# Filling the bank of z's second half ahead of its sum, in a gated graph layer on one Trainium2 core

## The chip, the core and the metric

The kernel runs on one core of a Trainium2 chip. The core has five engines that run side by side, each with its own instruction queue: TensorE (PE in the profile, with its weight loads shown as PEld), VectorE (DVE), ScalarE (ACT), GpSimd (POOL) and SyncE (SP, which here only issues transfers). Matmuls write to PSUM, a small memory of eight banks; one bank holds 128 rows of 512 fp32 numbers. Everything else works on SBUF or moves between SBUF and main memory through DMA.

The metric is the device time of one execution in microseconds; lower is better. Where several runs are shown, their median counts.

## The reference

`x` is 16 batches of 1024 nodes with 256 features, `adj` a 1024 x 1024 matrix in which about nine entries in a row are not zero. Cut to what matters:

```python
pre_u = einsum('bud,dk->buk', h_t, W1[:d])
pre_v = einsum('bvd,dk->bvk', h_t, W1[d:])
hidden = relu(pre_u[:, :, None, :] + pre_v[:, None, :, :] + b1)
S = sigmoid(einsum('buvk,ko->buvo', hidden, W2)[..., 0] + b2[0])
a_t = einsum('buv,bud->bvd', S * A_a, h_t)
m_t = einsum('uv,bud->bvd', A_m, h_t) * h_t
z_t = beta1 * h_t + beta2 * (einsum('bvd,de->bve', a_t, Wa) + ba) \
    + beta3 * (einsum('bvd,de->bve', m_t, Wm) + bm)
```

Here `A_a = A_m = adj`, and the three betas are inputs. So each edge (u, v) of each batch gets a gate S, the neighbours of v are summed once with the gate and once without, and z is made of three terms: beta1 h, two matrix products, and a bias row `beta2 ba + beta3 bm`, which the kernel calls `bias`.

## The kernel before

**Blocks and steps.** The batches are cut into NG = 4 groups of 4, the nodes v into NT = 8 tiles of 128. One pair (group, tile) is a block: BS = 32 blocks, in the order of the list `order`; the last group has blocks 24 to 31. A block takes T = 10 steps, so there are 320 steps, `n`, with `k, s = divmod(n, T)`: the block and the step in it. In a step 128 edges of the tile are worked on for the four batches of the group.

**One step.** GpSimd gathers table rows of the neighbours, pre_u and h, into one of eight buffers `fetched` (L518). PE spreads pre_v + b1 over the edges into a bank pair `pc` (`expand`, L615). DVE adds the two (`add`, L648), then in `gate` multiplies by W2 under the relu and sums, one instruction for each batch (L656, four a step). ACT makes the sigmoid (L659) and scales the left operand with it (L661; L625 prepares it). PE sums the neighbours into accumulators (`aggregate`, L673), two steps at a time. `expand(n + 2)` needs the bank that `add(n)` has read.

**Once in a block.** Other work is laid between the steps by `products` and its callees. They share two PSUM banks through `small`, which takes them in turn:

- `halves(k + 1)`: pre_v + b1 of the next block in two halves of two batches (L449, L445), at s = 1 and 3 from n = 10 on; ACT copies each half out twice (L482, L483).
- `rows`: table rows of a later group, at s = 8 and s = 2 of the next block, up to n = 222 (L445, copied out in L461).
- `turn_over`: ACT has copied an accumulator to `ev` (L681); PE transposes it (L691), ACT copies it to `LT` (L694). At s = 8, 9, 0 and 2.
- `block_end(k - 1)`: z of the block before, in two halves, `h = 0` at s = 4 and 5, `h = 1` at s = 6 and 7. A half starts with the bias row as a matmul with `start=True` (`add_row`, L449), then the products with w_a and w_m (L722). Then, in most blocks, ACT copies the bank over `LT` (L736), DVE computes `hb = beta1 hb + z` (L737), and SP writes `hb` out. For `h = 1` of the last group PE adds beta1 h instead, as a product with a scaled identity (`be1_eye`, L726), and ACT copies the sum out (L728).

`hb` is h of the block, in two halves, loaded by SP at s = 5 and s = 7 of the block itself into one of four buffers `h_blk` (L921). So z of block k is made while block k + 1 runs, and h for its second half is loaded seven steps before step 4 of that.

**What sets the order.** Each engine runs its instructions in the order in which the program issues them; `after(step, f)` puts a call off to the end of a later step (`do(n)`, after `gate(n)`). Up to n = 229 (`n < LAST`) `expand` and `products` come ahead of `add` and `gate` in a step; from n = 230 on they come behind. `ROOM` is 10, `LISTS` is 110: up to there the lists of edges are still being made (`lists`), which also take banks from `small` and copy a flag tile `few` on GpSimd (L335).

The bias row is kept in two forms: `bias`, and `bias_p`, split into two parts for the matmul whose other operand is `unit`, a 128 x 128 tile of ones.

Of the kernel before, what the change touches and what calls it, by code (L numbers as in the profile page):

```python
# [7 lines left out]
FP = mybir.dt.float32  # L8
FR = mybir.dt.float32r
I32 = mybir.dt.int32  # L10
AF = mybir.ActivationFunctionType
ALU = mybir.AluOpType
AX = mybir.AxisListType
P = 128
# [3 lines left out]
def kernel(  # L18
# [42 lines left out]
    nc = tc.nc  # L61
    B, N, D = x.shape
    NT = N // P
    DC = D // P
    GB = 4
    NG = B // GB
# [4 lines left out]
    E = TW * P  # L71
# [17 lines left out]
    def load_rows(src, n, name, engine=nc.scalar, at_=None):  # L89
        t = const.tile([P, n], FP, name=name) if at_ is None else at_  # L90
        engine.dma_start(t, bass.AP(tensor=src.tensor, offset=src.offset, ap=[[0, P], [1, n]]))
        return t
# [8 lines left out]
    def fixed(shape, name, dt=FP):  # L101
        return const.tile(shape, dt, name=name)
# [9 lines left out]
    upto = fixed([P, E], "upto")  # L112
# [3 lines left out]
    row = rows32[:, 0:1]  # L116
# [62 lines left out]
    slot, nth = upto, upto[:, :S]  # L179


    unit = fixed([P, P], "unit", FR)
    nc.vector.tensor_scalar(unit, upto[:, :P], 0.0, None, ALU.is_ge)
    edge = fixed([P, 1], "edge")
    nc.vector.tensor_scalar(edge, inw, 0.0, None, ALU.is_equal)

# [6 lines left out]
    bias_p = fixed([P, D], "bias_p", FR)  # L193
# [12 lines left out]
    main = ctx.enter_context(ExitStack())  # L206
# [6 lines left out]
    lst = ExitStack()  # L213
    lists_done = lst.close
    lst = lst.enter_context(tc.tile_pool(name="lst", bufs=1))
    psc = main.enter_context(tc.tile_pool(name="psc", bufs=2, space=bass.MemoryType.PSUM))
    psa = main.enter_context(tc.tile_pool(name="psa", bufs=1, space=bass.MemoryType.PSUM))
    psm = main.enter_context(tc.tile_pool(name="psm", bufs=2, space=bass.MemoryType.PSUM))

    def small(name):  # L220
        return psm.tile([P, 512], FP, name="misc")


    def aside(vt):
# [17 lines left out]
    def lists(vt):  # L242
# [7 lines left out]
        for c in range(0, N, N if vt < EARLY else N // 2):  # L250
            c = slice(c, c + (N if vt < EARLY else N // 2))
# [36 lines left out]
        for i in range(4):  # L288
            nc.tensor.matmul(pw[:, i:i + 1], sums[:, i].rearrange("p w q v -> p (w q v)"), R[:, 0:1],
                             start=True, stop=True)  # L290
# [36 lines left out]
        nc.vector.tensor_tensor(thr[:, vt:vt + 1], last, none, ALU.add)  # L327
        yield "op"
        RR = lst.tile([P, NW, RC], FP, name="RR", bufs=2)
        few = lst.tile([P, E], mybir.dt.uint8, name="few", bufs=2)  # L330
        yield "slot"
        for w, mine in enumerate((soon, late)):
            nc.vector.tensor_scalar(RR[:, w, :], R, mine, None, ALU.mult)
# [68 lines left out]
    def after(step, f):  # L402
        due.setdefault(step, []).append(f)
# [41 lines left out]
                nc.tensor.matmul(p[:, bb * D:(bb + 1) * D], hT[:, 2 * h + bb, i, :], wt[:, i, :],  # L445
                                 start=(i == 0 and not begun), stop=(i == DC - 1), skip_group_check=begun)

    def add_row(p, parts):
        nc.tensor.matmul(p, unit, parts.unsqueeze(1).to_broadcast([P, 2, D]),  # L449
                         start=True, stop=False, skip_group_check=True)  # L450

    def rows(k, tab=None):

# [14 lines left out]

    cuts = {}

    def halves(k):
        X = cuts[k] = big.tile([P, NW, GD], FR, name="X")
        low = one.tile([P, GD], FP, name="low")
        for h in range(2):
            step = yield
            c = slice(2 * h * D, (2 * h + 2) * D)
            p = small("p")
            add_row(p, b1_p)  # L480
            half_product(p, hTs[order[k]], w_v, h, True)
            nc.scalar.copy(X[:, 0, c], p)  # L482
            nc.scalar.copy(low[:, c], p)  # L483
        after(step + (2 if k else 1), lambda: nc.vector.tensor_tensor(low, low, X[:, 0, :].bitcast(FP), ALU.subtract))  # L484
        yield
        nc.scalar.copy(X[W:, 1, :], X[W:, 0, :].bitcast(FP))
        for w in range(NW):
            yield
            nc.scalar.copy(X[(1 - w) * W:(2 - w) * W, w, :], low[w * W:(w + 1) * W])  # L489
# [46 lines left out]
    spare = spare_.rearrange("p b c n -> p b (c n)")  # L536
# [9 lines left out]
    marks, pcs, accs, evs, hbs, LTs, lefts = {}, {}, {}, {}, {}, {}, {}  # L546
# [12 lines left out]
    parts = halves(0)  # L559
    for t, turns_ in enumerate(script):  # L560
        step = t - 100
# [148 lines left out]
    def block_end(k):  # L710

        g, vt = order[k]
        hb = hbs[k]
        for h in range(2):
            for i, wt in ((1, w_a), (0, w_m)):
                step = yield
                if i:
                    pz = small("pz")
                    add_row(pz, bias_p)
                for bb in range(2):  # L720
                    for c in range(DC):
                        nc.tensor.matmul(pz[:, bb * D:(bb + 1) * D], LTs[k][:, 2 * h + bb, i if bb else 1 - i, c, :], wt[:, c, :],  # L722
                                         start=False, stop=(i == 0 and c == DC - 1), skip_group_check=True)
            if h == 1 and g == NG - 1:
                for bb in range(2):
                    nc.tensor.matmul(pz[:, bb * D:(bb + 1) * D], be1_eye[0], hb[h][:, bb, :], start=False, stop=True,  # L726
                                     skip_group_check=True)
                nc.scalar.copy(hb[h], pz.rearrange("p (b d) -> p b d", b=2))  # L728
                b = g * GB + 2 * h
                after(step + 2, lambda hb=hb[h], b=b: nc.sync.dma_start(  # L730
                    out[b:b + 2, vt * P:(vt + 1) * P, :].rearrange("b p d -> p b d"), hb))
                continue
            z = pz.rearrange("p (b d) -> p b d", b=2)
            if step >= ROOM:
                z = LTs[k][:, 2 * h].rearrange("p k c n -> p (k c n)").rearrange("p (b d) -> p b d", b=2)
                nc.scalar.copy(z, pz.rearrange("p (b d) -> p b d", b=2))  # L736
            after(step + 1, lambda hb=hb[h], z=z: nc.vector.scalar_tensor_tensor(hb, hb, be1, z, ALU.mult, ALU.add))  # L737
            b = g * GB + 2 * h
            after(step + 2, lambda hb=hb[h], b=b: nc.sync.dma_start(
                out[b:b + 2, vt * P:(vt + 1) * P, :].rearrange("b p d -> p b d"), hb))  # L740
        del hbs[k], LTs[k]
# [120 lines left out]
    ROOM, MORE, LISTS = 10, 3, 110  # L862
    LAST = (BS - NT - 1) * T
# [18 lines left out]
    for n in range(total + 2):  # L882
        k, s = divmod(n, T)
        if n < total - 3:
            last_in = n - 1 if n % 2 or n < ROOM else done
        else:
            last_in = n
        while done < min(last_in, total):
            gather_in(done)
            done += 1  # L890
        if n % TW == 1 and n // TW + 1 < total // TW:
            load_mark(n // TW + 1)
        if n < LAST:
            expand(n + 2)
            if n >= ROOM:
                fill(n, False)
            products(n, k, s)
        if n + 1 < total:
            add(n + 1)
        if n < total:  # L900
            gate(n)
            if n + 1 < total:
                left_adj(n + 1)
        do(n)
        if s == 8 and ROOM <= n < LAST:
            turn_over(k, 0, 0, n)
        if n >= LAST and n + 2 < total:
            expand(n + 2)
        if n == 1:
            bias = load_rows(bm, D, "bias", nc.sync, spare[:, 1])  # L910
            ba_b = load_rows(ba, D, "ba_b", nc.sync, spare[:, 2])
            be1 = load_rows(beta1, 1, "be1", nc.sync)
            be2 = load_rows(beta2, 1, "be2", nc.sync)
            be3 = load_rows(beta3, 1, "be3", nc.sync)
            after(10, scale_late)
        if s in (5, 7) and k < BS - 1:
            h = s // 7
            hb = big.tile([P, 2, D], FP, name="h_blk", bufs=4)
            hbs.setdefault(k, []).append(hb)
            g, vt = order[k]  # L920
            nc.sync.dma_start(hb.rearrange("p b d -> p (b d)"),  # L921
                              table[g][vt * P:(vt + 1) * P, GD + 2 * h * D:GD + (2 * h + 2) * D])
        if n == total - 6:
            hbs[BS - 1] = hT_free.pop(0).rearrange("p b c n -> p b (c n)")
            for v, m, f in tails:
                for h, o in tail_rows(x, v, m, f):
                    nc.sync.dma_start(h, o)
        for i in advance.get(n, ()):
            next(made[i], None)
        if n in start_list:  # L930
            running.append([made[start_list[n]], True, n])
            piece_of(running[-1], n)
        if n < ROOM or n >= LAST:
            fill(n, False)
        if n >= LAST:
            products(n, k, s)
        if n == LISTS:
            assert not running and all(next(x, None) is None for x in made)
            lists_done()
            more = main.enter_context(tc.tile_pool(name="more", bufs=1))  # L940
            hT_free.extend(hT_places(more, MORE, NH))
# [120 lines left out]
```

## Time and profile before

| | |
|---|---|
| three runs | 1077.29, 1075.63, 1071.70 us; median 1075.63 |
| profiled execution | 1082.24 us, of it 1080.4 us from the first to the last instruction |
| mean granted TensorE clock | 0.990 |
| TensorE busy | 1020.1 us (94%) |
| VectorE busy | 1017.6 us (94%) |
| ScalarE busy | 862.6 us (80%) |
| GpSimd busy | 459.3 us (43%) |
| L737, beta1 h + z on DVE | 55 times, 743 ns each |
| L726, matmuls with be1_eye | 28 times, 7.2 us in all |
| L736, L728, copies of z on ACT | 55 and 7 times, 582 and 566 ns each |
| L449, bias row of z | 62 times, 24.6 us in all |

How to read it: a line of the profile names the kernel's line, the engine, the operation, and the tiles, `out<-in`; then a count and durations. The shares of busy time are means over the whole run. A matmul of fp32 operands appears as two passes, each with its own weight load, which is why 14 matmuls with `be1_eye` show as 28. Two views are used below: the windows, which give each engine's busy time in a stretch of the run, and the timeline, which lists instructions with their start and length, and in brackets how long the engine stood idle before them and what ended that.

### The profile page before, as it was taken

The page shows a single profiled execution, that of the slowest core. Times are in us where ns is not written, and L with a number is a line of the kernel's source. Part 1 is how long each engine was busy: PE and PEld are TensorE (multiplying, and loading weights), DVE is VectorE, ACT ScalarE, POOL GpSimd, SP SyncE. Part 2 cuts the span into 40 slices and gives each one's busy share as a digit, 9 for nine tenths or more (in the row PEclk, how much of TensorE's full clock was granted, in tenths as well). Part 3 has the DMA queues.
Part 4 walks back from the last instruction along what each step waited for, and adds up shares of the span by engine and source line. Part 5 has one row for each costly group of instructions (what it writes and reads, how often), then busy time and mean ns, then how long its engine had stood idle before and what let it go on. Part 6 is the DMA issues. An engine that isn't in the chain of part 4 may idle for free.

```text
span 1080.4 us, 24120 instructions
## 1 busy us (share of the span) xinstructions
PE 1020.1 (94%) x7673; PEld 731.3 (68%) x7673; DVE 1017.6 (94%) x3481; ACT 862.6 (80%) x2616; POOL 459.3 (43%) x456
## 2 busy tenths in 40 slices
PE   7777999999999999999999999999999999999996
PEld 6654676776666776677777767777766667666654
DVE  8687999998999999999999999999999999999993
ACT  3246787788888887898888888889889889999983
POOL 2666676555257334553333334333333333333330
PEclk9989999999999999999999999999999999999999
DMA  9999899999999999999999999999999999999991
GB/s 283 327 340 385 313 339 381 362 382 378 403 352 371 408 381 385 379 403 395 404 393 399 412 384 392 408 396 389 381 361 370 369 348 368 365 381 369 365 341 44
DMA packets 147752, 394.56 MB, mean 365 GB/s; under 512 B 18224, under 2 KB 94512, under 8 KB 111408
## 3 DMA queue, kind: packets, MB, share of 16 engines
q0 software_dynamic: 50544, 301.16, 70.9%
q1 hardware_dynamic: 83776, 78.66, 22.9%
q10 hardware_dynamic: 13296, 13.11, 3.5%
q8 instruction: 63, 1.03, 0.4%
q14 instruction: 73, 0.60, 0.1%
HBM read 396.93 MB, written 50.33 MB: 414 GB/s over the span
## 4 chain that ended last, share of the span: by engine, by line
PE 40%; DVE 34%; issue 10%; ACT 8%; DMA 5%; POOL 2%; another core or an unknown queue 0%; POOLq 0%; DVEq 0%; ACTq 0%
DVE fetched L656 16%; DVE fetched L648 12%; PE acc L673 10%; PE misc L722 10%; PE misc L445 9%; PE pc L615 7%; DMA fetched<-table,uidx 3%; PE misc L691 2%; ACT left L661 2%; DVE LT L705 1%; ACT X L489 1%; PE misc L449 1%; DVE low L484 1%; DVE h_blk L737 1%; DMA hT__635<-in_xT_dram 1%
## 5 line engine op out<-in xcount | busy, mean ns | idle before, releaser
L518 POOL DMA_INDIRECT fetched<-table,uidx x320 | 339.4, 1061 | 529.0 <-PE acc L673 389.0
L656 DVE SCALAR_TENSOR_TENSOR fetched<-fetched,w_b 128x256 f32<-128x256 f32 x1280 | 478.0, 419 | 0.0
L648 DVE TENSOR_TENSOR fetched<-fetched,pc 128x1024 f32<-128x1024 f32 x320 | 387.7, 1212 | 29.9 <-PE pc L615 19.4
L661 ACT ACTIVATE left<-left,gt 128x32 f32<-128x32 f32 (+1 forms) x1280 | 299.6, 305 | 10.4
L673 PE MATMUL acc<-fetched,left 128*32 128x256 f32 x4096 | 273.4, 385 | 6.3 <-ACT gt L659 3.7
L615 PE MATMUL pc<-X,mark 128*128 128x512 f32 x640 | 243.7, 462 | 10.9 <-DVE fetched L648 9.3
L673 PEld LDWEIGHTS acc<-fetched,left 128*32 128x32 f32 x4096 | 127.6, 109 | 112.1 <-issue 29.1
L615 PEld LDWEIGHTS pc<-X,mark 128*128 128x128 f32 x640 | 105.4, 189 | 88.9 <-issue 41.6
L659 ACT ACTIVATE gt<-sc,b_b 128x4 f32<-128x4 f32 x320 | 95.9, 300 | 46.7 <-DVE fetched L656 37.5
L722 PE MATMUL misc<-w_m,LT 128*128 128x256 f32 x496 | 117.3, 379 | 0.0
L722 PE MATMUL misc<-w_a,LT 128*128 128x256 f32 x496 | 117.2, 379 | 0.0
L445 PE MATMUL misc<-w_v,hT 128*128 128x256 f32 x448 | 107.6, 383 | 0.0
L722 PEld LDWEIGHTS misc<-w_a,LT 128*128 128x128 f32 x496 | 93.8, 189 | 15.3 <-issue 0.4
L722 PEld LDWEIGHTS misc<-w_m,LT 128*128 128x128 f32 x496 | 93.8, 190 | 15.1
L625 ACT ACTIVATE left<-onehot,val 128x64 f32<-128x64 bf16 (+1 forms) x320 | 102.9, 322 | 0.0
L385 POOL DMA_INDIRECT val<-in_adjT_dram,vidx x80 | 87.2, 1090 | 34.4 <-issue 20.4
L656 DVE DVE_READ_ACCUMULATOR fetched<-fetched,w_b 128x1 f32 x1280 | 100.7, 79 | 0.0
L691 PE MATMUL misc<-ident,ev 128*128 128x128 f32 x512 | 79.5, 278 | 18.5 <-issue 7.0
L445 PEld LDWEIGHTS misc<-w_v,hT 128*128 128x128 f32 x448 | 86.4, 193 | 14.3
L691 PEld LDWEIGHTS misc<-ident,ev 128*128 128x128 f32 x512 | 60.7, 141 | 45.7 <-ACT ev L681 15.2
L482 ACT CAST X<-misc 128x512 fp32r<-128x512 f32 x64 | 37.1, 580 | 55.2 <-PE misc L445 48.0
L445 PE MATMUL misc<-w_u,hT 128*128 128x256 f32 x320 | 76.6, 386 | 4.0 <-issue 3.8
(185 smaller groups left out, 1011.3 us busy)
## 6 DMA issues: line engine op xcount, KB each, us to landing
h_blk<-table SPq DMA_DIRECT2D x62, 256.0 KB
out_dram<-h_blk SPq DMA_DIRECT2D x62, 256.0 KB
hT<-in_xT_dram SPq DMA_DIRECT2D x28, 512.0 KB
table<-in_x_dram ACTq DMA_DIRECT2D x24, 512.0 KB
table<-tab SPq DMA_DIRECT2D x48, 256.0 KB
fetched<-table,uidx POOLq DMA_INDIRECT x320
table<-in_x_dram SPq DMA_DIRECT2D x8, 512.0 KB
table<-fetched SPq DMA_DIRECT2D x8, 512.0 KB
```

The lines of the kernel that those rows point to most:

```text
L385: nc.gpsimd.indirect_dma_start(out=val[:, i, j:j + 1], out_offset=None, in_=adj_flat, in_offset=bass.IndirectOffsetOnAxis(ap=vidx[:, i, j: ...
L445: nc.tensor.matmul(p[:, bb * D:(bb + 1) * D], hT[:, 2 * h + bb, i, :], wt[:, i, :], start=(i == 0 and not begun), stop=(i == DC - 1), skip ...
L518: nc.gpsimd.indirect_dma_start(out=fetched[at_slot[n]], out_offset=None, in_=table[g], in_offset=bass.IndirectOffsetOnAxis(ap=uidx[:, vt * ...
L615: nc.tensor.matmul(pcs[n][:, c], marks[n // TW][:, j * P:(j + 1) * P], cuts[k][:, w, c], start=True, stop=True)
L625: nc.scalar.activation(lefts[n][:, :m, 1::GB, :], onehot[:, i, o:o + m, :].unsqueeze(2).to_broadcast([P, m, GB // 2, V]), AF.Copy, scale=v ...
L648: nc.vector.tensor_tensor(t, t, pcs.pop(n), ALU.add)
L656: nc.vector.scalar_tensor_tensor(t[:, b, :], t[:, b, :], 0.0, w2_b, ALU.max, ALU.mult, accum_out=sc[:, b:b + 1])
L659: nc.scalar.activation(gt, sc, AF.Sigmoid, bias=b2_b)
L661: nc.scalar.activation(lefts[n][:, :m, 2 * b, :], lefts[n][:, :m, 1 + b // 2 * GB, :], AF.Copy, scale=gt[:, b:b + 1])
L673: nc.tensor.matmul(accs[h][b * 2 * V:(b + 1) * 2 * V, r, :], left[:, i, 2 * b - b % 2:2 * b - b % 2 + 2].rearrange("p k v -> p (k v)"), f[ ...
L691: nc.tensor.transpose(pt[:, r, :, c, :], ev[:, r, c * P:(c + 1) * P], ident)
L722: nc.tensor.matmul(pz[:, bb * D:(bb + 1) * D], LTs[k][:, 2 * h + bb, i if bb else 1 - i, c, :], wt[:, c, :], start=False, stop=(i == 0 and ...
```

## The change

`halves` gets a last part, `seed_z`. After the second half-product of block k, from step 111 on, it takes the bank of that half-product again and has it written: up to step 229 by DVE at the end of the next step, with beta1 h + bias; from step 230 on by ACT at once, with beta1 h. The tile is kept in the list `kept` until `block_end` takes it for `h = 1`. `small` now counts the banks itself in `turn_of`, so that a kept bank is passed by; the pool has two names with one buffer each in place of one name with two. `block_end` chooses by `filled` whether the bias row is added by a matmul, with or without `start`, and how the sum is finished.

Three changes free the memory: `unit` is one column, read 128 times; `few` has one buffer in place of two; `bias` gets a tile of its own, since it is now read to the end of block 22, where before it lay in a buffer that is used again.

```diff
-    unit = fixed([P, P], "unit", FR)
-    nc.vector.tensor_scalar(unit, upto[:, :P], 0.0, None, ALU.is_ge)
+    unit_ = fixed([P, 1], "unit", FR)
+    nc.vector.tensor_scalar(unit_, row, 0.0, None, ALU.is_ge)
+    unit = unit_.to_broadcast([P, P])
...
-    psm = main.enter_context(tc.tile_pool(name="psm", bufs=2, space=bass.MemoryType.PSUM))
-
-    def small(name):
-        return psm.tile([P, 512], FP, name="misc")
+    psm = main.enter_context(tc.tile_pool(name="psm", bufs=1, space=bass.MemoryType.PSUM))
+    turn_of, kept = [0], []
+
+    def small(name, bank=None):
+        if bank is None:
+            bank = turn_of[0] = 1 - turn_of[0]
+            if kept and kept[0][0] == bank:
+                bank = turn_of[0] = 1 - bank
+        return psm.tile([P, 512], FP, name=f"misc{bank}")
...
-        few = lst.tile([P, E], mybir.dt.uint8, name="few", bufs=2)
+        few = lst.tile([P, E], mybir.dt.uint8, name="few", bufs=1)
...
-    def add_row(p, parts):
+    def add_row(p, parts, start=True):
         nc.tensor.matmul(p, unit, parts.unsqueeze(1).to_broadcast([P, 2, D]),
-                         start=True, stop=False, skip_group_check=True)
+                         start=start, stop=False, skip_group_check=True)
...
+    def seed_z(k, step):
+        bank = turn_of[0]
+        pz = small("pz", bank)
+        kept.append((bank, pz))
+
+        def write():
+            z, hb = pz.rearrange("p (b d) -> p b d", d=D), hbs[k][1]
+            if step >= LAST:
+                nc.scalar.activation(z, hb, AF.Copy, scale=be1)
+            else:
+                nc.vector.scalar_tensor_tensor(z, hb, be1, bias.unsqueeze(1).to_broadcast([P, 2, D]), ALU.mult, ALU.add)
+        if step >= LAST:
+            write()
+        else:
+            after(step + 1, write)
+
...
             nc.scalar.copy(low[:, c], p)
+            if h == 1 and k > 1 and (step > LISTS):
+                seed_z(k - 2, step)
...
                 if i:
-                    pz = small("pz")
-                    add_row(pz, bias_p)
+                    filled = h == 1 and kept
+                    pz = kept.pop()[1] if filled else small("pz")
+                    if not filled or step >= LAST + 6:
+                        add_row(pz, bias_p, not filled)
...
-            if h == 1 and g == NG - 1:
+            by_eye = g == NG - 1 and not filled
+            if by_eye:
                 for bb in range(2):
                     nc.tensor.matmul(pz[:, bb * D:(bb + 1) * D], be1_eye[0], hb[h][:, bb, :], start=False, stop=True,
                                      skip_group_check=True)
+            b = g * GB + 2 * h
+            if by_eye or filled:
                 nc.scalar.copy(hb[h], pz.rearrange("p (b d) -> p b d", b=2))
...
-            z = pz.rearrange("p (b d) -> p b d", b=2)
-            if step >= ROOM:
-                z = LTs[k][:, 2 * h].rearrange("p k c n -> p (k c n)").rearrange("p (b d) -> p b d", b=2)
-                nc.scalar.copy(z, pz.rearrange("p (b d) -> p b d", b=2))
-            after(step + 1, lambda hb=hb[h], z=z: nc.vector.scalar_tensor_tensor(hb, hb, be1, z, ALU.mult, ALU.add))
-            b = g * GB + 2 * h
+            else:
+                z = pz.rearrange("p (b d) -> p b d", b=2)
+                if step >= ROOM:
+                    z = LTs[k][:, 2 * h].rearrange("p k c n -> p (k c n)").rearrange("p (b d) -> p b d", b=2)
+                    nc.scalar.copy(z, pz.rearrange("p (b d) -> p b d", b=2))
+                after(step + 1, lambda hb=hb[h], z=z: nc.vector.scalar_tensor_tensor(hb, hb, be1, z, ALU.mult, ALU.add))
...
-            bias = load_rows(bm, D, "bias", nc.sync, spare[:, 1])
+            bias = load_rows(bm, D, "bias", nc.sync)
```

More of the change, by code (lines that the diff above doesn't have):

```diff
@@ L727, in block_end @@
                                      skip_group_check=True)
+            b = g * GB + 2 * h
+            if by_eye or filled:
                 nc.scalar.copy(hb[h], pz.rearrange("p (b d) -> p b d", b=2))
-                b = g * GB + 2 * h
-                after(step + 2, lambda hb=hb[h], b=b: nc.sync.dma_start(
-                    out[b:b + 2, vt * P:(vt + 1) * P, :].rearrange("b p d -> p b d"), hb))
-                continue
-            z = pz.rearrange("p (b d) -> p b d", b=2)
-            if step >= ROOM:
-                z = LTs[k][:, 2 * h].rearrange("p k c n -> p (k c n)").rearrange("p (b d) -> p b d", b=2)
-                nc.scalar.copy(z, pz.rearrange("p (b d) -> p b d", b=2))
-            after(step + 1, lambda hb=hb[h], z=z: nc.vector.scalar_tensor_tensor(hb, hb, be1, z, ALU.mult, ALU.add))
-            b = g * GB + 2 * h
+            else:
[4 more added lines that the diff above has]
+                after(step + 1, lambda hb=hb[h], z=z: nc.vector.scalar_tensor_tensor(hb, hb, be1, z, ALU.mult, ALU.add))
             after(step + 2, lambda hb=hb[h], b=b: nc.sync.dma_start(
```

## The prediction

> **What bounds the kernel now.** I read the busy time by stage first, because the page's shares (PE 94%, DVE 94%) average two regimes. The windows view cuts whole blocks (ten steps each) out of the run: blocks 16, 19, 27 and 29. Columns after the stretch: length, then busy us (and instructions) of PE, PEld, DVE, ACT, POOL, then clock, DMA share, GB/s.
>
> ```profile
> 591.70:621.90 30.20, 30.13 (x234) 21.95 (x233) 28.98 (x97) 26.36 (x82) 10.83 (x10) 1.00 1.03 410
> 683.30:713.50 30.20, 30.13 (x234) 21.83 (x233) 29.00 (x96) 26.36 (x82) 10.63 (x10) 1.00 1.02 400
> 918.90:947.10 28.20, 27.55 (x228) 19.60 (x223) 28.20 (x95) 25.63 (x80) 10.38 (x10) 1.00 0.96 360
> 975.30:1003.50 28.20, 27.59 (x228) 19.68 (x224) 28.20 (x95) 25.59 (x80) 10.12 (x10) 1.00 0.98 366
> ```
>
> In blocks 12 to 22 PE is idle 0.07 us of 30.2 and DVE 1.2 us: PE sets the period. In blocks 25 to 30 DVE is never idle and PE lacks 0.6 us: DVE sets it. The waits view agrees: in 471.4 to 773.7 DVE L648 waits 11.9 us for PE L615, in 862.4 to 1031.7 it waits for nothing.
>
> Then the timeline at the end of block 15, PE's weight loads and ACT's copies (start us, length):
>
> ```profile
> 590.27 0.59 ACT L736 COPY LT<-misc 128x512 f32<-128x512 f32 x1 [0.15 <-PE misc L722]
> ...
> 595.72 0.58 ACT L681 COPY ev<-acc 128x512 f32<-128x512 f32 x1
> ```
> ```profile
> 590.31 1.71 PEld L445 LDWEIGHTS misc<-w_u,hT__6826 128*128 128x128 f32 x8
> 592.04 0.57 PEld L691 LDWEIGHTS misc<-ident,ev 128*128 128x128 f32 x4
> ...
> 595.54 0.30 PEld L615 LDWEIGHTS pc<-X,mark 128*128 128x128 f32 x2
> 596.35 0.42 PEld L691 LDWEIGHTS misc<-ident,ev 128*128 128x128 f32 x4 [0.50 <-ACT ev L681]
> 596.94 0.16 PEld L673 LDWEIGHTS acc<-fetched,left 128*32 128x32 f32 x8 [0.17 <-issue]
> ```
>
> Two paths leave the end of z's second half (590.23). PE goes on with the next table rows (L445) at once, in the other bank, and reaches the transposes at about 595.86. ACT copies z out (L736), then works without a gap up to the copy of ev, which ends at 596.30. PE waits 0.5 us for it. So here ACT's path, not PE's own work, is the longer one, by half a microsecond.
>
> The same place in a DVE-bound block (end of 27):
>
> ```profile
> 944.12 0.84 PEld L726 LDWEIGHTS misc<-h_blk,be_eye 128*128 128x128 f32 x4
> 944.99 0.41 PEld L615 LDWEIGHTS pc<-X,mark 128*128 128x128 f32 x2
> 945.43 0.59 PEld L691 LDWEIGHTS misc<-ident,ev 128*128 128x128 f32 x4
> 946.19 1.45 PEld L673 LDWEIGHTS acc<-fetched,left 128*32 128x32 f32 x32 [0.17 <-issue]
> ...
> 950.30 0.42 PEld L691 LDWEIGHTS misc<-ident,ev 128*128 128x128 f32 x4 [1.04 <-ACT ev L681]
> 950.88 0.16 PEld L673 LDWEIGHTS acc<-fetched,left 128*32 128x32 f32 x8 [0.17 <-issue]
> ```
>
> **The change, part by part.**
>
> *What it does when built.* `filled = h == 1 and kept` names the list `kept` itself, not a truth value. The next line pops its only entry, so every later `not filled` is true. Hence the bias matmul is issued for both halves with start=True, over the seed; in the last group both halves, not one, go through be1_eye; the other blocks keep copy and L737. The instruction order of the built kernel says the same: 62 bias_p matmuls as before, be1_eye matmuls 14 to 28 (two passes each), L737 55 to 48, and beside them 12 new DVE and 8 new ACT writes into misc. The seeds are extra work that is thrown away. [...]
>
> *DVE seeds, blocks 11 to 22.* 128x512, two SBUF inputs, PSUM output. No row writes PSUM from DVE; nearest are L737 (0.743 us, 0.665 to the next start) and twice L648 per element, 1.21. I take 0.665 by form. It stands after step 4's gates, where DVE runs some 3.6 us ahead (L648 of 609.33 ends at 610.55 and frees the bank that PE takes at 614.23), and is hidden in the 1.2 us of idle; 0 us. Without that cover: 12 x 0.665 = 8.0 us. It also reads h four steps earlier than L737 did; the load for block 16 is issued at 591.5, its last packet ends at 609.7, and the seed would be due at 609.3. Up to a microsecond there, once; the others land 2.3 us or more before.
>
> *ACT seeds, blocks 23 to 30.* Nearest L728, 0.566 us. They follow the copies at 934.66, ahead of a gap of 0.67 us in which ACT waits for DVE: 0 us. Uncovered: 8 x 0.57 = 4.6.
>
> *The bank.* This is what I think costs most. `seed_z` keeps the bank of the second half-product for z, and turn_of stays on the other one. So the first `small` after z takes z's own bank, where before it took the other. It must wait until ACT has copied z out. The trace has this very wait once, in block 9, where the bookkeeping of the lists had turned the parity:
>
> ```profile
> 402.98 0.59 ACT L736 COPY LT<-misc 128x512 f32<-128x512 f32 x1 [0.67 <-PE misc L722]
> ...
> 403.61 1.59 PEld L445 LDWEIGHTS misc<-w_u,hT 128*128 128x128 f32 x8 [0.65 <-ACT LT L736]
> ```
>
> The weight load itself waits, and starts 0.05 after the copy. At 590.31 it would start at 590.86 + 0.05 = 590.91: 0.60 late. Eight loads after a wait take 1.63 us to the next one, against 1.73 unhindered, so the transposes come 0.49 late and reach the ev wait at 595.86 + 0.49 = 596.35: just when ev is ready. ACT's path starts at z's end and is not moved. What is left is the order in which loads and matmuls overlap: the matmul before the transposes ends 0.48 later (596.76), transposes end 0.44 behind it as at 595.38 to 595.82, and L673 loads at 597.12 instead of 596.94: 0.18. Blocks 11 to 22: 12 x 0.18 = **2.2 us**. Bounds: 0 if ACT's path swallows all, 12 x 0.60 = 7.2 if nothing is swallowed.
>
> [...] The row at 403.61 shows the load held with its matmul. [...]
>
> *Blocks 25 to 30 (z of 24 to 29).* DVE loses one L737: 28.20 - 0.665 = 27.54. PE gains four loads of be1_eye for the first half, 0.863 from the first to what follows (944.12 to 944.99). PE's own period now: the wait at 950.30 costs 0.83 (without it the transposes would end 0.44 after the matmul before them, which ends at 949.68, and L673 loads 0.07 ahead of that end: 950.05, not 950.88), so 28.20 - 0.83 = 27.37. New: 27.37 + 0.86 = 28.23, and the bank wait: z ends 945.36, copied 945.40 to 945.98, transposes load at 946.03 instead of 945.43, end 0.66 later at 946.69 instead of 946.26: 0.43. PE's period is 28.66. DVE's own way round (L648 to the gates 22.5, ACT to the end of the copy 2.1, PE to the next L615 3.2, hand-over 0.2) is 28.0, below. ev is then ready at 949.5 and no longer waited for. 28.66 - 28.20 = 0.46, six times: **2.8 us**. Bounds: 0.03 x 6 = 0.2 with the bank wait swallowed, and with only the 0.62 us of idle as slack (0.86 + 0.60 - 0.62) x 6 = 5.0.
>
> *Blocks 23, 24, 31.* In 23 and 24 ACT copies late (832.53, against a load at 830.41), but L615's next result is due at 836.12 and would be there at 835.8: 0. Block 31 gets be1_eye for both halves without a seed: 0.86 on PE, 0.47 of it ahead of a wait for ACT: 0.4; bounds 0 and 0.9.
>
> *The rest.* `unit` as one broadcast column: 0.18 us of DVE at 4.9 us goes; the load with step 0 has no row, all loads of 128 columns take 0.187 to 0.193, so 0. `few` with one buffer: the closest copies are 42.2 and 52.5, and the transfers between them end at 50.1: 0, 2.4 us spare. `bias` in a tile of its own: the same load and sum.
>
> **Sum:** 2.2 + 2.8 + 0.4 = 5.4 us on a span of 1080.4 (execution 1082.2). The runs' median, 1075.63, is 0.6% lower than that execution; the blocks are the same work, so 1075.6 + 5.4 = 1081.0. 0.5% (5.4 us) is about what can be told from no change, so the forecast sits on that line.
>
> **Rivals.**
> - *The bank wait passes on in full*: each block's PE path moves by 0.60 because ACT's path, which waits for PE at 590.27, moves too. 7.2 + 5.0 + 0.9 = 13.1: 1088.7. For: PE is idle only 0.07 us. Against: the 0.50 us wait for ev. 0.20.
> - *All is swallowed*: 0 + 0.2 + 0.4: 1076.2. For: ACT's path is the longer one now. Against: matmul order, and 0.86 more on PE against 0.83 of slack. 0.20.
> - *VectorE becomes the bound in 11 to 22* (slower): a seed that finds h late stops the gates behind it. Spare are 1.2 - 0.665 = 0.55 plus the 0.2 that PE loses, so from 0.75 us a block on it decides; at 1.5 us it adds 0.75 x 12 = 9.0: 1090. For: 609.7 against 609.3. Against: the other loads. 0.07.
> - *It does what its words say*: PE saves 0.23 (L449's pitch) and pays 0.18 in 12 blocks, -0.6; in 25 to 30 be1_eye only changes halves, PE 27.37 + 0.43 = 27.80, -0.4 x 6; -1 in 23 and 24: 1071.6. Against: the built order. 0.03.
>
> **How the numbers follow.** Forecast 0.50, own range 1078 to 1084, half of it under the line and half over. Slower by over 0.5%: 0.25 + 0.20 + 0.07 = 0.52. Within: 0.25 + 0.20 - 0.01 for scatter = 0.44. Faster: 0.03 + 0.01 = 0.04. The range goes from just under the swallowed case to the case in full: 1075 to 1089.
>
> **What would show it.** Right: in blocks 11 to 22 the first load after z waits some 0.6 us for ACT's copy of z, the ev wait shrinks from 0.5 to near 0, and the period goes from 30.13 to 30.3; in 25 to 30 DVE is idle again, about 1.1 us, and the period is 28.66; be1_eye matmuls 56; no wait before the DVE seeds. Wrong: periods of 30.7 (full), a period of 28.2 (swallowed), DVE waiting for a load of h_blk, or fewer bias_p matmuls than before.

## The result, and the profile after

The changed kernel is slower: 1092.75 us against 1077.02 us, medians of six runs each on one chip, ratio 1.0149 with a 95% interval of 1.0117 to 1.0181. That is 16 us where the prediction had 5.4, and outside its range of 1075 to 1089 us. The profiled execution of the changed kernel took 1095.94 us, of it 1094.1 from the first to the last instruction.

First the places that the prediction spoke of. The windows view of the changed kernel, blocks 16, 27 and 29, with the same columns as before:

```profile
600.00:630.20 30.20, 29.98 (x233) 21.85 (x232) 29.55 (x97) 26.35 (x82) 11.04 (x10) 1.00 1.02 407
927.30:957.20 29.90, 28.77 (x224) 20.48 (x224) 27.69 (x92) 26.11 (x81) 10.11 (x10) 1.00 0.95 346
986.00:1014.70 28.70, 28.48 (x224) 20.54 (x224) 27.78 (x94) 26.28 (x81) 9.92 (x10) 1.00 0.98 363
```

PE still sets the period in block 16, and now idles 0.2 us of it. In block 29 the period is 28.70 in place of 28.20, and DVE idles 0.9 us where it idled none: PE has taken over. (Block 27 has one disturbance more; 26, 28, 29 and 30 take 28.72, 28.75, 28.69 and 28.69.)

The timeline of the changed kernel at the end of block 15, and then at the end of block 28:

```profile
597.58 0.58 ACT L762 COPY LT<-misc 128x512 f32<-128x512 f32 x1 [0.15 <-PE misc L748]
598.21 1.59 PEld L451 LDWEIGHTS misc<-w_u,hT__6832 128*128 128x128 f32 x8 [0.64 <-ACT LT L762]
...
603.03 0.58 ACT L705 COPY ev<-acc 128x512 f32<-128x512 f32 x1
603.68 0.59 PEld L715 LDWEIGHTS misc<-ident,ev 128*128 128x128 f32 x4
```
```profile
984.24 0.84 PEld L753 LDWEIGHTS misc<-h_blk,be_eye 128*128 128x128 f32 x4
985.52 0.59 ACT L757 COPY h_blk<-misc 128x512 f32<-128x512 f32 x1
986.16 0.42 PEld L715 LDWEIGHTS misc<-ident,ev 128*128 128x128 f32 x4 [0.65 <-ACT h_blk L757]
```

Both show the wait for z's own bank. At 598.21 the load starts 0.05 us after ACT's copy (597.58 + 0.58), with 0.64 us of idling ahead of it, and the wait of 0.50 for `ev` further on is gone. At 986.16 the transposes wait 0.65 in the same way.

Now what the prediction did not have. PE's waits over the whole run of the changed kernel (line waited at, what for: us in all, times, longest) have two lines that the run before lacks at this size:

```profile
PE misc L451 <- DVE from L306: 7.9, 2, 5.1
PE misc L715 <- DVE from L306: 5.1, 1, 5.1
```

They fall in blocks 3, 6 and 9, while the lists of edges are still made. The timeline of the changed kernel in block 3 (PE, and one line of DVE):

```profile
177.85 0.95 PE L295 MATMUL misc<-R,sums 128*128 128x1 f32 x8
178.97 1.89 PE L451 MATMUL misc<-w_v,hT 128*128 128x256 f32 x8
...
186.21 0.16 DVE L306 TENSOR_TENSOR from<-misc,from 128x1 f32<-128x1 f32 x1
186.42 3.78 PE L451 MATMUL misc<-w_u,hT__1792 128*128 128x256 f32 x8 [5.10 <-DVE from L306]
```

L295 is the small product `pw` that the lists need. It holds one of the two banks until DVE has read it, in four instructions that make `from` and `first`, of which L306 is the last, at 186.21. (The profile's "wait for `from`" is the wait for this last one.) The half-product at 178.97 takes the other bank, and is soon copied out. The table row's product is next by strict turn on the bank of `pw`, though ACT has copied the other one out by 181.97. It waits 5.10 us. The same place in the kernel before:

```profile
182.86 0.95 PE L289 MATMUL misc<-R,sums 128*128 128x1 f32 x8
183.98 1.89 PE L445 MATMUL misc<-w_v,hT 128*128 128x256 f32 x8
188.53 1.99 PE L445 MATMUL misc<-w_u,hT__1791 128*128 128x256 f32 x8 [2.20 <-issue]
...
191.22 0.16 DVE L300 TENSOR_TENSOR from<-misc,from 128x1 f32<-128x1 f32 x1
```

There the third product runs at 188.53, 2.7 us ahead of the last read of `pw`. It can't be in that bank: the pool of two buffers under one name gave it the other one, and so passed the held one by.

The wait has a second price. In the changed kernel the eight matmuls at 186.42 take 3.78 us, where eight of the same size take 1.89 at 178.97. The windows view gives the granted clock (the column after POOL) around the wait:

```profile
172.30:185.00 12.70, 8.97 (x62) 6.36 (x60) 12.70 (x48) 9.77 (x32) 8.24 (x8) 1.00 1.02 383
186.40:190.20 3.80, 3.78 (x9) 2.96 (x10) 0.30 (x2) 0.00 (x0) 0.00 (x0) 0.50 0.57 193
190.20:200.00 9.80, 9.80 (x82) 6.39 (x81) 6.77 (x26) 6.59 (x20) 4.61 (x5) 0.88 0.79 245
```

Half the clock for 3.8 us and 0.88 for 9.8 more: 3.8 x 0.5 + 9.8 x 0.12 = 3.1 us of PE's work, lost on top of the wait.

A third thing is one seed. DVE's timeline in block 13 of the changed kernel:

```profile
527.35 0.76 DVE L487 SCALAR_TENSOR_TENSOR misc<-h_blk,be,bias 128x512 f32<-128x512 f32 x1 [5.89 <-DMA h_blk<-table]
```

The other eleven DVE seeds and the eight on ACT wait for no transfer.

### The profile page after: what moved, and what is told of

It reads as the page before. It is cut to its first block, busy times and chain, and to the rows that moved or that the text cites. A ratio compares the mean times of both kernels' runs of the same rounds, so it can differ in the third digit from the quotient of the medians.

```text
span 1094.1 us, 24217 instructions
## 1 busy us (share of the span) xinstructions
PE 1029.7 (94%) x7701; PEld 742.8 (68%) x7701; DVE 1022.1 (93%) x3486; ACT 868.4 (79%) x2624; POOL 462.3 (42%) x456
## 4 chain that ended last, share of the span: by engine, by line
PE 57%; DVE 23%; DMA 9%; issue 5%; ACT 4%; POOL 1%; ACTq 0%; SPq 0%; DVEq 0%; POOLq 0%
PE acc L697 15%; PE misc L451 14%; PE misc L748 12%; PE pc L639 9%; DVE fetched L680 9%; DVE fetched L672 7%; DMA fetched<-table,uidx 4%; PE misc L715 3%; DMA h_blk<-table 3%; PE misc L455 2%; ACT left L685 1%; DVE LT L729 1%; DVE low L508 1%; DMA hT__635<-in_xT_dram 1%; ACT LT L762 1%
## 5 line engine op out<-in xcount | busy, mean ns | idle before, releaser
L697 PE MATMUL acc<-fetched,left 128*32 128x256 f32 x4096 | 270.2, 386 | 3.4 <-ACT left L685 3.1
L639 PE MATMUL pc<-X,mark 128*128 128x512 f32 x640 | 244.2, 463 | 18.7 <-DVE fetched L672 18.6
L680 DVE DVE_READ_ACCUMULATOR fetched<-fetched,w_b 128x1 f32 x1280 | 109.5, 86 | 0.0
L715 PEld LDWEIGHTS misc<-ident,ev 128*128 128x128 f32 x512 | 63.3, 144 | 36.7 <-DVE from L306 5.6
```

The costliest lines, as they stand in the source:

```text
L639: nc.tensor.matmul(pcs[n][:, c], marks[n // TW][:, j * P:(j + 1) * P], cuts[k][:, w, c], start=True, stop=True)
L680: nc.vector.scalar_tensor_tensor(t[:, b, :], t[:, b, :], 0.0, w2_b, ALU.max, ALU.mult, accum_out=sc[:, b:b + 1])
L697: nc.tensor.matmul(accs[h][b * 2 * V:(b + 1) * 2 * V, r, :], left[:, i, 2 * b - b % 2:2 * b - b % 2 + 2].rearrange("p k v -> p (k v)"), f[ ...
L715: nc.tensor.transpose(pt[:, r, :, c, :], ev[:, r, c * P:(c + 1) * P], ident)
```

## The experiments

Each was run in five rounds beside the kernel before, whose median was 1076.5, 1075.9 and 1076.7 us in the three sets. Ratios are to the kernel before on the same chip.

| kernel | us | ratio, 95% interval |
|---|---|---|
| changed | 1092.75 | 1.0149 [1.0117, 1.0181] |
| small_only | 1082.78 | 1.0071 [1.0040, 1.0103] |
| noseed | 1085.56 | 1.0087 [1.0053, 1.0121] |
| eye2 | 1079.83 | 1.0038 [1.0011, 1.0064] |
| pool_seeds | 1079.29 | 1.0024 [0.9999, 1.0048] |
| e1_held | 1083.08 | 1.0053 [1.0026, 1.0080] |
| e5_turn | 1085.53 | 1.0087 [1.0062, 1.0111] |
| held_turn | 1078.55 | 1.0016 [0.9988, 1.0045] |
| e6_earlyh | 1088.53 | 1.0103 [1.0072, 1.0135] |
| pool_noseed | 1076.73 | 1.0000 [0.9973, 1.0027] |
| e4_bool | 1087.09 | 1.0098 [1.0063, 1.0133] |
| pool_bool | 1072.15 | 0.9958 [0.9929, 0.9987] |
| pool_bool_earlyh | 1073.48 | 0.9961 [0.9937, 0.9984] |

Block periods in us (start of the add in step 0 to that of the next block; for block 31 to the end of DVE's last instruction), read from the timelines of one execution each:

| block | before | changed | small_only | e1_held | e5_turn | held_turn | pool_bool |
|---|---|---|---|---|---|---|---|
| 3 | 35.20 | 40.15 | 39.21 | 33.68 | 39.47 | 34.82 | 33.67 |
| 6 | 33.59 | 35.41 | 35.02 | 33.56 | 35.39 | 33.64 | 33.61 |
| 10 | 34.01 | 36.34 | 36.34 | 34.02 | 36.33 | 33.13 | 33.13 |
| 13 | 30.66 | 35.73 | 30.42 | 36.58 | 32.80 | 30.77 | 34.00 |
| 20 | 30.13 | 30.21 | 30.26 | 30.23 | 30.13 | 30.16 | 29.90 |
| 29 | 28.24 | 28.69 | 28.20 | 28.69 | 28.27 | 28.27 | 27.61 |
| 31 | 41.95 | 43.84 | 41.94 | 43.25 | 42.84 | 42.86 | 42.33 |

### The turn alone: small_only

The kernel before, with only the strict turn:

```diff
-    psm = main.enter_context(tc.tile_pool(name="psm", bufs=2, space=bass.MemoryType.PSUM))
+    psm = main.enter_context(tc.tile_pool(name="psm", bufs=1, space=bass.MemoryType.PSUM))
+    turn_of = [0]
     def small(name):
-        return psm.tile([P, 512], FP, name="misc")
+        bank = turn_of[0] = 1 - turn_of[0]
+        return psm.tile([P, 512], FP, name=f"misc{bank}")
```

> The kernel before with nothing but the new counting of the two banks (two names with one buffer each, taken strictly in turn). Theory A (the lists' small product keeps its bank until VectorE has read it; the pool passed such a bank by, the strict turn runs into it): TensorE waits for VectorE's 'from' instructions, over 10 us in all against 1 to 2 before, mostly in blocks 3, 6 and 9, the granted clock falls below 0.985, blocks 12 to 30 keep their periods (30.1 and 28.2 us), and the time is 4 to 8 us over before. Rival B (the early blocks of the changed kernel were slower by chance): no such waits, within 3 us of before.

It costs 7.6 us (0.71% of 1076.5) with no seed, no be1_eye and no kept bank. The timeline has the same waits, and behind them a granted clock of 0.50 and 0.54 over 3.5 us (3.78 and 1.11 us for what takes 1.89 and 0.60 to 0.66):

```profile
185.25 3.78 PE L447 MATMUL misc<-w_u,hT__1791 128*128 128x256 f32 x8 [5.09 <-DVE from L302]
281.67 1.11 PE L693 MATMUL misc<-ident,ev 128*128 128x128 f32 x4 [5.14 <-DVE from L302]
```

Blocks 12 to 30 are as before. Half of the loss thus comes from a part of the change whose cost the prediction never worked out.

### No seeds: noseed

The changed kernel without the call of `seed_z`; no bank is kept, and the bias matmul starts every sum.

```diff
-            if h == 1 and k > 1 and (step > LISTS):
-                seed_z(k - 2, step)
```

> The changed kernel without seeds: the bank isn't kept, nothing is written ahead; the strict turn, be1_eye for both halves of the last group, unit, few and bias stay. Theory A with my own sums for the rest: small_only plus 0 to 1 us (blocks 25 to 30 at 28.2 to 28.3 us: TensorE 28.23, VectorE 27.54), blocks 12 to 22 at 30.1, no VectorE wait for h_blk; 4 to 9 us over before, so 7 to 11 us under the changed kernel. Rival (be1_eye is the cost): blocks 25 to 30 stay at 28.7, 3 us more than small_only.

The waits for `from` stay (5.1, 5.1 and 2.9 us). Block 29 comes back to 28.26, so be1_eye for both halves costs 0.02 to 0.06 a block there (28.20 to 28.24 before) and the rest of the 0.45 is z's bank. Seeds and z's bank together are 1.0149 - 1.0087 = 0.6%, some 6.7 us. Over before that leaves 9.4 us, just outside the 4 to 9 that I expected.

### be1_eye for both halves: eye2

The kernel before, with one condition changed:

```diff
-            if h == 1 and g == NG - 1:
+            if g == NG - 1:
```

> The kernel before with be1_eye for both halves of the last group. My sum: TensorE's period 27.37 + 0.86 = 28.23, VectorE's 27.54, so 28.2 us as before and 0 to 1 us in all. Rival (0.62 us of idle is all the slack there is): 28.4 to 28.5, 1.5 us and more; with 0.4 us for block 31 about 2 us.

By its ratio 1 to 7 us; by its periods less: 0.05 to 0.1 in most of blocks 25 to 30, and 0.9 in block 31 (42.86 for 41.95). pool_noseed below has the same edit and reads 1.0000. Between 0 and 4 us it stays open.

### The seeds with the old pool: pool_seeds

The changed kernel with the pool of before. No second tile is taken: the seed goes into the half-product's own tile, which holds its bank until z is done.

```diff
-    def seed_z(k, step):
-        bank = turn_of[0]
-        pz = small("pz", bank)
-        kept.append((bank, pz))
+    def seed_z(k, step, pz):
+        kept.append((0, pz))
```

> The changed kernel with the old pool of two buffers: the seed goes into the half-product's own tile, which the pool then keeps. Every bank is as in the kernel before, and the seeds are still overwritten. Theory A: no waits for 'from' beyond those of before, no wait for the copy of z, so blocks 12 to 22 at 30.1 and 25 to 30 at 28.2 to 28.3; what is left is be1_eye (0 to 1 us) and a VectorE wait for a late h_blk (0 to 6 us, in one block): 0 to 7 us over before. Rival C (the seeds' own time on VectorE counts): 12 x 0.665 = 8 us and more, periods of 30.8 in blocks 12 to 22.

With the banks as before, all seeds, the 28 more passes of be1_eye and the thrown-away work come to 0.24%, which the interval can't tell from nothing. No wait of PE's matmuls for `from` is over 0.6 us, and block 29 takes 28.27. Its profile has a wait of another kind, in block 13, to which pool_noseed returns.

### The held bank passed by: e1_held

The first experiments could still be read as a matter of which bank comes first. This one keeps the strict turn, changes its parity, and passes by the bank of `pw` alone:

```diff
-            if kept and kept[0][0] == bank:
+            if kept and kept[0][0] == bank or bank in taken:
                 bank = turn_of[0] = 1 - bank
...
         pw = aside(vt)
+        if vt >= EARLY - 1:
+            taken.append(turn_of[0])
...
         nc.vector.tensor_tensor(from_, pw[:, 3:4], from_, ALU.max)
+        taken.clear()
```

> The changed kernel, but `small` also passes by the bank of the lists' product `pw` until VectorE's `from` instructions have read it, as the old pool did. Theory A (in the list phase the strict turn runs into that bank): PE's waits for `from` (5.1 us in block 3, 5.1 in block 6, 2.8 in block 9) go, blocks 3, 6 and 10 come back to about 33.9, 33.6 and 33.3 us, and the time is 1085 us, 5 to 9 under the changed kernel, ratio to before 1.006 to 1.010; what is left is the bank of z and be1_eye. Rival B (it is not the held bank but that the order of banks differs at all, or the clock): the waits stay or turn up at other products, and the time stays at 1091 to 1094.

1.0149 becomes 1.0053: about 10 us back. The timeline in block 3 shows the row's product 4.2 us ahead of the last read of `pw`:

```profile
177.00 0.95 PE L297 MATMUL misc<-R,sums 128*128 128x1 f32 x8
178.12 1.89 PE L454 MATMUL misc<-w_v,hT 128*128 128x256 f32 x8
181.17 1.99 PE L454 MATMUL misc<-w_u,hT__1792 128*128 128x256 f32 x8 [0.70 <-ACT low L508]
...
185.37 0.15 DVE L308 TENSOR_TENSOR from<-misc,from 128x1 f32<-128x1 f32 x1
```

Eight matmuls take 1.99 us; the granted clock from 171.5 to 205.2 us is 1.00. Block 3 gives back 6.5 us: the wait is 4.4 shorter (0.70 for 5.10), and the 3.1 us that the clock had cost are more than the 2.1 left. The rival falls.

### z's bank alone: e5_turn

```diff
-                    pz = kept.pop()[1] if filled else small("pz")
+                    if filled:
+                        turn_of[0], pz = kept.pop()
+                    else:
+                        pz = small("pz")
```

> The changed kernel, but when the kept bank is taken for z, the turn moves with it, so that the first `small` after z gets the other bank and not z's own. Blocks 0 to 10 stay as in the changed kernel (waits for `from` of 5 us and all). Theory A: PE no longer waits for ACT's copy of z; blocks 25 to 30 go from 28.7 to 28.27, blocks 11 to 22 from 30.2 to 30.1, together 4 to 5 us with blocks 23, 24 and 31: 1088 us. Rival B (the last 7 us between the kernel without seeds and the changed one are the seeds' own cost, not z's bank): periods stay at 28.7 and 30.2, and the time stays at 1091 to 1094.

1.0087, some 6.7 us under the changed kernel, more than the 4 to 5 that I expected. The windows view, block 29:

```profile
976.00:1004.30 28.30, 28.30 (x227) 20.39 (x226) 27.81 (x94) 26.33 (x81) 10.20 (x10) 1.00 0.98 370
```

28.27 in place of 28.69, and block 20 back to 30.13. Blocks 26, 28, 29 and 30 give back 0.43 to 0.62 us each, and 20 to 22 give back 0.1 to 0.2 each. Not all of the difference between these two profiles is z's bank: of the 4.9 us in blocks 11 to 22, 2.9 lie in block 13, where the seed waited 2.9 us for h and not 5.9; and the 0.9 us in 23 and 24 together (58.9 to 58.0) are not there in e1_held, whose z's bank is taken in the same way and which needs 57.7.

### Both repairs of the banks: held_turn

> The changed kernel with both repairs of the banks: `small` passes by the bank of `pw` until `from` has read it, and the turn moves with the kept bank. If the two costs are separate places of the run, they add: the list phase gave back 9.6 thousandths and the turn 6.2, so 1.0149 - 0.0158 = 0.999, at most 1.003: 1075 to 1079 us, what is left being be1_eye for both halves and the late h in block 13. Rival (the two repairs reach the same wait, or the second one is scatter): 1.005 as with the first alone, 1081 to 1083.

1.0016, as the sum of the two demands; no difference from before can be told. The two places are separate, and they hold nearly all of the loss. With `pw`'s bank passed by in both, e1_held and held_turn differ by z's bank alone: 1.0053 - 1.0016 = 0.4%, 4 us.

### h loaded early: e6_earlyh

```diff
-        if s in (5, 7) and k < BS - 1:
-            h = s // 7
+        for h in range(2 * (s == 5 and k < BS - 1)):
```

> The changed kernel, but both halves of h are loaded at s = 5, not the second at s = 7. Theory A (the seed reads h before it has landed, once, in block 13): the wait of 5.9 us before the seed goes, block 13 comes from 35.7 back to some 30 to 31, and the time is 3 to 6 us under the changed kernel, 1087 to 1090. Rival B (SP's queue is behind at 500 us whatever stands in it): the wait moves to the load of hT, which now stands behind that of h, block 13 stays at 33 to 40 and the time at 1091 to 1095.

1.0103, 4 to 5 us under the changed kernel, though the intervals overlap. The windows view of block 13, first in the changed kernel, then here:

```profile
504.80:540.50 35.70, 32.08 (x243) 22.67 (x238) 29.81 (x100) 26.73 (x82) 10.90 (x10) 0.95 1.02 387
```
```profile
498.90:528.60 29.70, 29.49 (x231) 21.56 (x224) 29.70 (x100) 25.90 (x80) 10.55 (x10) 1.00 1.04 406
```

DVE idles 5.9 us in the first and not at all in the second. The late seed also cost PE its clock (0.95). That a seed waits for h here is no chance: 5.9, 6.7, 2.9 and 3.4 us in block 13 of the changed kernel, e1_held, e5_turn and e4_bool, and 6.6 us, a block later, in held_turn.

### The old pool without seeds: pool_noseed

The edits of pool_seeds to the pool, and no call of `seed_z`: of the change only be1_eye, `unit`, `few` and `bias` are left.

> The changed kernel with the old pool and without the call of seed_z: what is left of the change is be1_eye for both halves in the last group, the column `unit`, one buffer for `few` and a tile for `bias`. Theory A (the seeds bring late transfers in block 13, be1_eye costs 0.07 a block): block 13 at 30 to 31 with no wait over 1.5 us for hT, blocks 25 to 30 at 28.27, 1076 to 1080 us, 1.000 to 1.004. Rival B (the waits of block 13 belong to the earlier arrival at 490 us, not to the seeds): block 13 at 34 to 40 here too.

1.0000: those four edits cost nothing that can be measured. But my theory of block 13 missed: it takes 41.5 us here, without any seed. PE waits for hT, as in pool_seeds; PE's waits in the whole run of this kernel, then of that one:

```profile
PE misc L447 <- DMA hT<-in_xT_dram: 9.0, 1, 9.0
```
```profile
PE misc L447 <- DMA hT<-in_xT_dram: 9.3, 1, 9.3
```

Around 490 to 500 us SP's queue is behind in kernels that load h at s = 7: the issue of the second half of h in block 12, where most such issues take 0.3 to 0.5 us, takes 8.7 us before and in the changed kernel, 12.7 in noseed and 18.0 in small_only. With the seeds, the first to feel it is often the seed, which needs h four steps earlier than L737 did; without them it can be PE, which needs hT, or nobody (30.2 and 30.4 in eye2 and small_only). Which it is differs from kernel to kernel, and one execution of each is not enough to say why.

### As the words say: e4_bool, pool_bool, pool_bool_earlyh

```diff
-                    filled = h == 1 and kept
+                    filled = h == 1 and bool(kept)
```

e4_bool has this edit alone, pool_bool has it with the pool of pool_seeds, pool_bool_earlyh also has both halves of h loaded at s = 5.

> The changed kernel with `filled` as a truth value, so that the seed stands: no bias matmul for the second half up to step 235, be1_eye for the first half alone in the last group, no copy and no beta1 h + z for the second halves. Strict turn as in the changed kernel. By the prediction's terms: blocks 11 to 22 30.13 - 0.23 + 0.18 = 30.1; blocks 25 to 30 27.8 to 28.0 in place of 28.7; the list phase keeps its 7.6 us. Sum: 1076.5 + 7.6 - 0.5 - 1.8 = 1082, ratio 1.003 to 1.008, some 10 us under the changed kernel. Rival: the thrown-away seeds and matmuls cost nothing beside the banks, then it stays above 1088.

1.0098, not 1.003 to 1.008: 5 us under the changed kernel, half of what I expected. Both waits for a bank are still there, and the second grew. The timeline at the end of block 28:

```profile
977.24 0.56 ACT L757 COPY h_blk<-misc 128x512 f32<-128x512 f32 x1
977.85 0.42 PEld L715 LDWEIGHTS misc<-ident,ev 128*128 128x128 f32 x4 [1.27 <-ACT h_blk L757]
```

Without be1_eye after it z ends sooner, at 976.55, but ACT still has the left operand of a gate to scale (0.96 us from 976.13) and copies z at 977.24. The load waits 1.27 where it waited 0.65, and block 29 takes 28.53.

> The change as its words say, `filled` as a truth value, with the old pool of two buffers under one name (the seed is put into the second half-product's own tile). Theory A (the idea itself pays once the banks are left as they were): banks free as before, no waits for `from`, no wait for the copy of z. Blocks 11 to 22 at 29.9 (30.13 less the bias matmul's 0.23), blocks 25 to 30 at 27.5 to 28.0, together -4 to -6 us: 1071 to 1073, ratio 0.994 to 0.997. Rival B (VectorE or ScalarE sets the period as soon as PE gives way, or transfers come late as in block 13): periods as before, 30.1 and 28.2, and the time is 1075 to 1079, not told from before.

The ratio is 0.9958: faster than before, by 1 to 8 us, and some 20 us under the changed kernel. The windows view, blocks 19 and 28:

```profile
674.20:704.10 29.90, 29.83 (x233) 21.70 (x232) 28.95 (x98) 26.23 (x82) 11.05 (x10) 1.00 1.01 394
934.80:962.40 27.60, 26.64 (x212) 19.05 (x204) 27.60 (x94) 26.19 (x81) 10.15 (x10) 1.00 0.99 373
```

29.90 is 30.13 less the 0.23 of the bias matmul, as expected. 27.60 is 28.20 less L737 (27.54 with its 0.665), with DVE never idle: DVE sets it as before. Blocks 25, 28 and 29 take that; 26, 27 and 30 take 28.1 to 28.6 in this execution.

In e4_bool and pool_bool the second halves have no bias matmul with `start=True`, and z comes out right: the products added to what DVE or ACT had written. A matmul had just written every element of that bank in both kernels (`misc<-b_p,unit`, 128x512, of the half-product); over such a bank the seed counted.

> The change as its words say with the old pool, and both halves of h loaded at s = 5. If late h is a real term, block 13 goes from 34.0 to about 30 and the time to 1067 to 1070 us, 0.991 to 0.994. Rival (in that kernel the wait of block 13 is PE's, 4.3 us for hT, which then stands behind h in SP's queue): 1072 to 1077, 0.996 to 1.000.

Block 13 came from 34.00 to 29.95, as the first theory has it, but the median did not follow (0.9961 and 0.9958). What a single execution shows of block 13 is no measure of the runs' median here, and the expectation missed.

## Why the prediction was right and wrong

**Right: what the change does when built.** After the change be1_eye has 56 passes, L763 (L737 before) 48 calls, and the bias matmul 62; the seeds are written and overwritten. On DVE they take 0.665 us to the next start, as forecast (0.76 in length), on ACT 0.69 in length for 0.566, and pool_seeds shows that their time is hidden (1.0024, block 29 at 28.27). Had the words been believed, the sum would have been negative.

**Right: z's own bank, in place and size.** Forecast 0.18 a block in 11 to 22 and 0.46 in 25 to 30. Measured 30.2 to 30.3 for 30.1 in blocks 20 to 22, and 28.69 to 28.75 for 28.20 in 26, 28, 29 and 30. There the bank is 0.43 (28.69 less 28.26 in noseed), which is the 0.43 read off the timeline of before. In blocks 11 to 22 the wait for `ev` took up the rest, as argued, and the loads were held with their matmuls (598.21, 986.16), as the row at 403.61 had it. The rivals of 30.7 and of 28.2 both fall. Blocks 23 and 24 were forecast at 0: e1_held has 28.86 and 28.85 there, no more than before (29.72 and 28.88), though the load waits 2.2 us for z's copy in both. In the changed kernel the clock fell after the first of these waits (0.70 in the 3.5 us behind it), and block 24 took 30.06.

**Wrong: "The rest" was costed at nothing.** It went through `unit`, `few` and `bias` (0, and pool_noseed bears that out), but not through the pool. The turn's own replacement was weighed only where a bank is kept, after step 110. It acts from the first product on. Of the 16 us, e1_held gives back 10.3 (0.96%), and small_only loses 7.6 by this alone. The working even came past the evidence: the row at 403.61, where a load waits for the copy of z in block 9, was put down to parity that "the bookkeeping of the lists had turned". What it shows is the old pool as it passes by the bank of `pw` and takes z's bank, which is about to come free. Two more lines of the kernel before say so: DVE starts to read `pw` only after 403.61, and the next product in turn waits for the last of these reads.

```profile
404.51 0.27 DVE L294 TENSOR_SCALAR from<-misc,base,low__102 128x1 f32<-128x1 f32 x1
...
406.25 0.66 PE L691 MATMUL misc<-ident,ev 128*128 128x128 f32 x4 [0.64 <-DVE from L300]
```

In the changed kernel the product at the place of 403.61 waits 2.85 us for `from`. The name of what holds the other bank at 403.61 would have given both the wait and its length.

**Wrong in size: the late h.** The prediction allowed "up to a microsecond there, once", in block 16, and 2.3 us or more to spare elsewhere. It came in block 13, at 5.9 us, and e6_earlyh puts it at 4 to 5 us of the total. The step took the end of the last packet, counted in the trace, for the time at which h may be read: in block 16, 18.2 us after the issue (609.7 less 591.5). The seed of block 13 was released 27.7 us after SP began to issue its load (499.67 to 527.35). Where the trace gives a landing of that same load, it is 18.3 us in pool_seeds, 18.7 in eye2 and 24.8 in small_only. Why the queue is behind there stays open. The rival that had DVE wait for h was the right mechanism, in one block instead of twelve.

**Wrong in size: block 31.** Forecast 0.4, measured 1.9. Of this 0.9 is be1_eye (eye2), the upper bound. Some 0.4 is the last of the six waits for z's bank, forecast under blocks 25 to 30: by the count used here they fall at the start of blocks 26 to 31 (e1_held has 43.25 with it, held_turn 42.86 without). The other 0.6 no run explains.

**Wrong: the rival "as its words say"** was given 1071.6 and 3 in 100. The price fits pool_bool (1072.15), but only with the old pool; with the turn it is 1087. The term left out there is the same one.

**A trap in the comparison.** Span against span, the list phase hides its loss: block 11 starts at 441 us in the profile of before and at 444 in that of the changed kernel. But that execution of before was slow early on. Its block 1 took 40.23 us, where all other kernels take 35.6 to 36.6, and with the same banks eye2, pool_seeds and pool_bool reach block 11 at 430 to 433. Counted from the first add, blocks 0 to 10 take 378 to 382 us in the six kernels that take the banks of the list phase strictly in turn, and 369 to 371 in the seven others besides before (375). One profile is one execution; a phase's length needs a second kernel with that phase unchanged.

## What to carry to other kernels

A pool that hands out what comes free and a fixed turn are the same only while all holders release in order; before such a swap, list every tile that takes a buffer and who frees it last, in all phases, and not only in the one that the change is about. Price a new wait on TensorE with the clock after it: here a wait of 5.1 us cost 3.1 more. And where an expression such as `h == 1 and kept` stands for a truth value, work out which of the two the built program has before costing anything.

## What the hardware showed

In these profiles the granted TensorE clock fell after waits that I had taken for harmless. From 130 to 1040 us of all fourteen, PE has 24 idle gaps of 2.8 to 9.3 us; in the 3.5 us after each of them the granted clock was 0.50 to 0.67. Of 12 gaps of 1.6 to 2.2 us, ten left it at 1.00. Two did not, such as this one at the end of block 23 in the changed kernel, with 0.70 behind it:

```profile
839.69 0.66 PE L715 MATMUL misc<-ident,ev 128*128 128x128 f32 x4 [1.79 <-ACT LT L762]
```

Two of the shortest of the 24 are the wait of 2.85 us before 407.24 in the changed kernel, with 0.55 behind it, and that of 2.88 us before 406.26 in noseed, with 0.52. The matmuls took as much longer: eight of them 3.78 us at 0.50 (186.42 in the changed kernel) for 1.89 at 1.00 (178.97).
